# Edge attributes carried through the edge factors' matmul, in a graph block on one core

## The chip, the cores and the metric

One NeuronCore of a Trainium2 chip runs the whole kernel. The metric is the device time in microseconds (us) of one execution, as the median of several. All data are float32 unless a row says otherwise.

## The reference

A graph block of the PaiNN kind, with a residual and a layer norm around it. There are 1250 nodes of 512 numbers (a vector part of 3 x 128, a scalar part of 128) and 40000 edges, sorted by `dst`. `edge_attr` has three numbers for each edge, `edge_weight` is its length r.

```python
x_j = x[src]                                          # a row of 512 for each edge
v_j, s_j = x_j[:, :384].reshape(E, 128, 3), x_j[:, 384:]
s_j = silu(s_j @ W1 + b1) @ W3 + b3                   # 128 -> 384
rbf = sqrt(2 / R) * sin(n * pi * r / R) / r           # n = 1..20
edge_basis = (rbf * cutoff(r)) @ W2 + b2              # 20 -> 384
s1, s2, s3 = split(s_j * edge_basis)
v_msg = v_j * s1[..., None] + s3[..., None] * edge_attr[:, None, :]
x = x + segment_sum(concat([v_msg, s2]), dst)         # first half
x_j = x[src]                                          # second half: a function of
...                                                   # the new x[src] alone, with
x = x + segment_sum(concat([v_2, scal_2]), dst)       # U, V, Wu1, Wu2
return layernorm(x_in + x)
```

## The kernel before

**Preparation.** A node's share of an edge message does not depend on the edge, so the kernel first makes a table in DRAM with one row for each node (`make_rows`, `table_row`; L590 stores it), and a message is the gathered row times the edge's 384 factors. The start also brings indices and weights into the layout that the loop needs. A count of edges that fall out of their windows (L374, cast to an integer at L375, read by the branch at L389) decides between the fast path, `windowed`, and a general one; all here is `windowed`. The attributes are loaded by `load_edges` (L378, issued on the DMA queue of the sync engine, SP; the store's rows name the tile `counts`) and brought to edges-on-partitions by three `turn_attr`: four TensorE transposes each (L284) and a ScalarE copy (L285) into `sh.carried`, which holds four numbers an edge: three attributes and the edge's place in its window of destinations. `sh.attr` is a view of the first three.

**Tiles.** The sorted edges are cut in 79 chunks of 512. Four chunks are a group `g` (20 groups); batch `t` = (group, i) takes the i-th tile of 128 edges of each of the four chunks. There are 80 batches, of which the last two or three are smaller. Each chunk's edges end in a window of 32 destination nodes, so that a sum over edges is a matmul with a one-hot of 128 edges x 32 nodes.

**One batch.**
- GpSimd: `gather(t + 3)`, four indirect DMAs (L743) that bring 4 x 128 table rows into one of five buffers, which the profile names `more` (three of them) and `nodes` (two). The first of the four waits, by a manual dependency, until TensorE has made the factors of batch t + 1.
- TensorE: `edge_factors(t + 1)` (L893) multiplies the transposed basis (`basis_t`, 21 rows: 20 radial functions and a one for the bias) by `w2_sb`, into four PSUM banks `eb`. There is one set of these banks.
- VectorE: `messages(t)`: L903 multiplies the scalar and s3 parts of the gathered rows by the factors in place, L905 the vector part, and with L905 the factors have been read for the last time. Then come the tasks listed under `amid` (among them `make_basis`, L801, `low_counts`, L1017, and one part of `make_turns`, L766); `make_pair` (L926: a one-hot of numbers); and for the batch ahead `make_hot(t + 1)` (L834: the window's one-hot) and `make_spread(t + 1)` (L846: one-hot times the three attributes of `sh.attr`, 3 x 32 columns a tile).
- TensorE: `add_messages(t - 1)` sums with `hot` (L942) and `spread` (L948) into the bank `agg`; `count_links` (L971) multiplies ScalarE's one-hots of the source (L858, L868) by `pair` into the bank `adj`, a count of links between nodes which the second half uses in place of a gather. Spare columns of `adj` hold constants that L766 and L801 read.

Between these, every eighth batch starts the node-wise second half for 128 nodes (products with U, V, Wu1, Wu2), and every fourth closes a group.

**Order.** Each engine runs its instructions in the order of the program. The loop over `t` calls `messages(t)`, the lists `first`, then `add_messages`, `count_links`, `early`, `edge_factors(t + 1)`, `gather(t + 3)`, `mid`, `late`, `dve`. A task is put in a list with a batch and a rank by `at(list, batch, rank, task)`. `count_links` stands ahead of the next `edge_factors` on TensorE, or, in batches with an `amid` task that do not follow a group's last batch (`behind`), after them. A batch after a group's last one, with a `make_basis` among its `amid` tasks too, comes at every eighth: batches 4, 12, 20 and so on.

```python
for t in range(...):
    messages(t)                  # L903, L905, amid, L926, L834, L846
    run(first, t)
    add_messages(t - 1)
    if t not in behind: count_links(t - 1)
    run(early, t)
    made = edge_factors(t + 1)
    gather(t + 3, made)
    if t in behind: count_links(t - 1)
    run(mid, t); run(late, t); run(dve, t)
```

`make_basis` makes the basis of one group ahead (L801), `turn_basis` transposes it (L810) and copies it out of PSUM on ScalarE (L815).

## Time and profile before

| what | value |
| --- | --- |
| median of 3 runs | 491.45 us (491.45, 495.45, 490.73) |
| profiled execution, its own time | 487.85 us |
| its span in the trace | 486.0 us |
| busy: TensorE, VectorE, ScalarE, GpSimd | 402.4, 429.6, 374.4, 344.1 us |
| moved by DMA | 123.29 MB, mean 254 GB/s |
| granted TensorE clock, mean | 0.954 of full speed |

The span is the time from the first to the last record of the profiled execution; its own time is 1.85 us longer. In the rows of the profile `L846 DVE ... x81 | 44.1, 546 | 2.7` is a line of the program, its engine (PE is TensorE, DVE VectorE, ACT ScalarE, POOL GpSimd, SP the sync engine), the number of instructions, their busy time in us, the mean of one in ns, and the idle time in front of them. A row that starts with two numbers is one instruction: its start in us from the start of the span, and its duration in us; what stands in brackets is how long its engine idled ahead of it, and what ended that.

### The profile page before, as it was taken

The page shows a single profiled execution, that of the slowest core. Times are in us where ns is not written, and L with a number is a line of the kernel's source. Part 1 is how long each engine was busy: PE and PEld are TensorE (multiplying, and loading weights), DVE is VectorE, ACT ScalarE, POOL GpSimd, SP SyncE. Part 2 cuts the span into 40 slices and gives each one's busy share as a digit, 9 for nine tenths or more (in the row PEclk, how much of TensorE's full clock was granted, in tenths as well). Part 3 has the DMA queues.
Part 4 walks back from the last instruction along what each step waited for, and adds up shares of the span by engine and source line. Part 5 has one row for each costly group of instructions (what it writes and reads, how often), then busy time and mean ns, then how long its engine had stood idle before and what let it go on. Part 6 is the DMA issues. An engine that isn't in the chain of part 4 may idle for free.

```text
span 486.0 us, 11224 instructions
## 1 busy us (share of the span) xinstructions
PE 402.4 (83%) x4257; PEld 231.4 (48%) x4257; DVE 429.6 (88%) x670; ACT 374.4 (77%) x955; POOL 344.1 (71%) x368
## 2 busy tenths in 40 slices
PE   8537766878869787787888889899899899999992
PEld 6323333444435345444534544554465555555781
DVE  5679799969998998998999899899989989988594
ACT  4486486669859977977986897899789789967672
POOL 9467677777777777777777777777777777781530
PEclk9956798989999999999998999999999999999996
DMA  8988788888888888888888888888888888889023
GB/s 245 325 227 254 228 245 251 252 265 257 276 265 279 276 265 269 269 271 261 269 271 254 290 263 279 264 286 272 282 260 274 270 276 284 264 268 317 6 91 129
DMA packets 37842, 123.29 MB, mean 254 GB/s; under 512 B 7196, under 2 KB 9774, under 8 KB 37778
## 3 DMA queue, kind: packets, MB, share of 16 engines
q0 software_dynamic: 25728, 104.47, 68.9%
q1 hardware_dynamic: 10850, 17.35, 10.7%
q8 instruction: 35, 0.57, 0.5%
q10 hardware_dynamic: 1200, 0.66, 0.5%
q14 instruction: 29, 0.24, 0.2%
HBM read 112.94 MB, written 9.51 MB: 252 GB/s over the span
## 4 chain that ended last, share of the span: by engine, by line
PE 31%; DVE 31%; DMA 13%; POOL 9%; issue 8%; ACT 6%; DVEq 1%; POOLq 0%; SPq 0%
DMA more<-table,src_i 8%; DVE more L905 7%; POOL more L743 6%; PE eb L893 6%; DVE nodes L905 5%; DVE more L903 4%; PE agg L942 4%; DVE nodes L903 4%; PE begun L1346 3%; POOL nodes L743 3%; PE agg L948 3%; PE adj L971 3%; DMA nodes<-in_x_dram 2%; DMA nodes<-table,src_i 2%; ACT one L868 2%
## 5 line engine op out<-in xcount | busy, mean ns | idle before, releaser
L743 POOL DMA_INDIRECT more<-table,src_i x189 | 187.7, 993 | 65.2 <-issue 48.3
L743 POOL DMA_INDIRECT nodes<-table,src_i x124 | 122.9, 991 | 37.8 <-issue 33.5
L868 ACT ACTIVATE one<-one,weight,src_f 128x128 f16<-128x128 f16 x313 | 128.5, 482 | 0.2
L893 PE MATMUL eb<-w_sb,basis_t 21*128 21x384 f32 x614 | 74.1, 551 | 41.7 <-DVE more L905 30.1
L858 ACT ACTIVATE one<-number,low 128x128 f16<-128x128 f16 x313 | 99.8, 392 | 6.9 <-PE adj L971 6.9
L905 DVE TENSOR_TENSOR more<-more,eb 128x1536 f32<-128x1536 f32 (+2 forms) x48 | 81.8, 1705 | 0.0
L903 DVE TENSOR_TENSOR more<-more,eb 128x1024 f32<-128x1024 f32 (+2 forms) x48 | 57.0, 1189 | 15.7 <-PE eb L893 7.3
L893 PEld LDWEIGHTS eb<-w_sb,basis_t 21*128 21x128 f32 x614 | 24.7, 188 | 62.8 <-DVE more L905 39.6
L942 PE MATMUL agg<-more,hot 128*32 128x512 f32 x378 | 54.6, 643 | 0.0
L905 DVE TENSOR_TENSOR nodes<-nodes,eb 128x1536 f32<-128x1536 f32 x30 | 52.5, 1749 | 0.0
L971 PE MATMUL adj<-pair,one 128*128 128x160 f16 x313 | 36.1, 238 | 19.0 <-DVE basis L801 19.0
L948 PEld LDWEIGHTS agg<-more,spread 128*32 128x32 f32 x1134 | 35.3, 116 | 31.9 <-issue 31.0
L903 DVE TENSOR_TENSOR nodes<-nodes,eb 128x1024 f32<-128x1024 f32 x30 | 36.5, 1218 | 11.9 <-PE eb L893 10.0
L846 DVE TENSOR_TENSOR spread<-hot,carried 128x384 f32<-128x384 f32 (+1 forms) x81 | 44.1, 546 | 2.7
L948 PE MATMUL agg<-more,spread 128*32 128x128 f32 x1134 | 42.6, 284 | 0.0
L971 PEld LDWEIGHTS <-one 128*128 128x128 f16 x313 | 22.6, 101 | 35.0 <-issue 33.0
L926 DVE TENSOR_TENSOR pair<-number,column 128x640 f16<-128x640 f16 (+1 forms) x81 | 39.1, 484 | 0.0
L942 PE MATMUL agg<-nodes,hot 128*32 128x512 f32 x248 | 34.1, 605 | 0.0
L948 PEld LDWEIGHTS agg<-nodes,spread 128*32 128x32 f32 x744 | 22.2, 110 | 19.2 <-issue 19.2
L1346 PE MATMUL begun<-upper,cast 128*128 128x512 f32 x57 | 27.8, 487 | 0.4 <-ACT cast L1337 0.4
L815 ACT COPY basis_t<-work 128x512 f32<-128x512 f32 x20 | 11.7, 583 | 20.4 <-PE work L810 20.3
L948 PE MATMUL agg<-nodes,spread 128*32 128x128 f32 x744 | 26.8, 273 | 0.0
(289 smaller groups left out, 687.0 us busy)
## 6 DMA issues: line engine op xcount, KB each, us to landing
table<-more SPq DMA_DIRECT2D x10, 320.0 KB
more<-table,src_i POOLq DMA_INDIRECT x189
spilled<-begun SPq DMA_DIRECT2D x10, 256.0 KB
more<-spilled SPq DMA_DIRECT2D x2, 1280.0 KB
node_x<-in_x_dram SPq DMA_DIRECT2D x35, 64.0 KB
nodes<-table,src_i POOLq DMA_INDIRECT x124
out_dram<-more SPq DMA_DIRECT2D x7, 256.0 KB
nodes<-in_x_dram POOLq DMA_DIRECT2D x2, 768.0 KB
```

The source lines that it names most:

```text
L743: got = nc.gpsimd.indirect_dma_start(out=rows_t[:n, j, :], out_offset=None, in_=sh.table1, in_offset=bass.IndirectOffsetOnAxis(ap=sh.src_i ...
L846: nc.vector.tensor_mul(spread[t][:m, js], hots[t][:m, js, None, :].to_broadcast(shape), sh.attr[:m, g, e : e + n, :, None].to_broadcast(sh ...
L858: nc.scalar.activation(onehots[t][:, j, :], number[:, :P], AF.Abs, bias=low[:, e : e + 1])
L868: nc.scalar.activation(one, one, AF.Relu, scale=less[:, e : e + 1], bias=worth[:, e : e + 1])
L893: made = nc.tensor.matmul(made_in[t][:, j, :V], turned[g][rows, i, :], sh.w2_sb[rows, :], start=True, stop=True,)
L903: nc.vector.tensor_mul(msg[:m, js, V:], msg[:m, js, V:], factors_of(t, js)[:m, :, C:V])
L905: nc.vector.tensor_mul(msg[:m, js, :V].rearrange("p t (k c) -> p t k c", k=3), msg[:m, js, :V].rearrange("p t (k c) -> p t k c", k=3), fac ...
L926: nc.vector.tensor_tensor(pair[:m, js, :].rearrange("p t (l h) -> p t l h", h=2), number[:m, : PARTS * WIN].rearrange("p (l h) -> p l h", ...
L942: nc.tensor.matmul(agg[j * WIN : (j + 1) * WIN, :], hots[t][:, j, :], msg[:, j, :width], start=(i == 0), stop=False, skip_group_check=True,)
L948: nc.tensor.matmul(agg[j * WIN : (j + 1) * WIN, c * C : (c + 1) * C], spread[t][:, j, c, :], msg[:, j, width:], start=False, stop=(i == la ...
L971: nc.tensor.matmul(to[:, :, at : at + WIN], one[:m, j, :], pair[:m, j, :].rearrange("e (p n) -> e p n", n=WIN), start=(i == 0 and j == js[ ...
L1346: nc.tensor.matmul(acc, casts[a, b], rows[:, a, :], start=(start and a == first and k == 0), stop=(stop and a == end - 1 and k == 1),)
```

## The change

- `w2_sb` gets four more columns, `V` to `V + 3`. The rows of features 21 to 24 of each tile hold a one there on the diagonal (`own`), zeros elsewhere.
- `carry(g)` copies the group's `sh.carried` into columns 21 to 24 of the basis, on ScalarE. With that, `edge_factors` has 25 rows in place of 21, 388 columns in place of 384, and the attributes come out behind the factors, in the same PSUM banks.
- `make_spread(t)` reads them there. It stands right behind L905 of its own batch, ahead of `amid`, and no longer a batch ahead; two buffers in place of three. `make_hot` stays a batch ahead.
- At the start the load of the attributes waits until the misses have been counted, and `turn_attr`, with the first `carry`, comes ahead of the first `turn_basis` and of most of the second pass of `floors` (`by_half`).

```diff
-    w2_sb = const.tile([P, V], F32)
+    w2_sb = const.tile([P, V + CARRY], F32)
...
+    nc.vector.scalar_tensor_tensor(
+        own, part, float(-N_RBF - 1), place[:, 2:3], op0=ALU.add, op1=ALU.subtract
+    )
...
-    nc.vector.tensor_copy(missed_i, missed)
+    counted = nc.vector.tensor_copy(missed_i, missed)
     nc.vector.tensor_copy(sh.src_i, sh.src_f)
+    nc.vector.tensor_scalar(w2_sb[:, V:], lane[:, :CARRY], own, None, op0=ALU.is_equal)
     by_tile(ps_front, local_r, 0, 1, sh.local, 1)
-    load_edges(sh.att_r, edge_attr, 3)
+    whole = nc.sync.dma_start(sh.att_r[:full, :], ...)
+    tc.add_manual_dep(
+        whole.ins, counted.ins.name, ...,
+        reason="so that the last rows land first",
+    )
...
+        def carry(g):
+            nc.scalar.copy(basis[:, :, N_RBF + 1 : N_RBF + 1 + CARRY], sh.carried[:, g])
...
         def make_spread(t):
             g, i = batches[t]
+            spread[t] = pool.tile([P, CPG, 3, WIN], F32, name="spread", bufs=2)
+            clear_rest(t, spread[t])
...
                     hots[t][:m, js, None, :].to_broadcast(shape),
-                    sh.attr[:m, g, e : e + n, :, None].to_broadcast(shape),
+                    factors_of(t, js)[:m, :, V : V + 3, None].to_broadcast(shape),
...
-                rows = slice(j * FEAT, j * FEAT + N_RBF + 1)
+                rows = slice(j * FEAT, j * FEAT + N_RBF + 1 + CARRY)
                 made = nc.tensor.matmul(
-                    made_in[t][:, j, :V], turned[g][rows, i, :], sh.w2_sb[rows, :],
+                    made_in[t][:, j, : V + CARRY], turned[g][rows, i, :], sh.w2_sb[rows, :],
...
+            make_spread(t)
             run(amid, t)
             make_pair(t)
-            if t == 0:
-                make_spread(0)
             if t + 1 < NT:
                 make_hot(t + 1)
-                make_spread(t + 1)
...
             at(amid, base + 2, 5, make_basis, g)
+            at(early, base + 2, 7, carry, g)
...
                 at(amid, base + 4, 4, make_basis, g + 1)
+                at(early, base + 4, 7, carry, g + 1)
...
+        next(by_half)
...
+        for k in range(3):
...
+            turn_attr(k, to.rearrange("p (i e) -> p i e", i=TPC))
+        carry(0)
         turn_basis(0)
         for _ in by_half:
             pass
...
-        for k in range(3):
...
-            turn_attr(k, to.rearrange("p (i e) -> p i e", i=TPC))
```

What the orders show. First VectorE, in a batch that makes a basis (batch 12, the first two rows its products; the last row is the next batch's first product). Before:

```order
L903 TENSOR_TENSOR more<-more,eb_384 128x4x256
L905 TENSOR_TENSOR more<-more,eb_384 128x4x384
L801 TENSOR_TENSOR basis<-turn,adj 128x16x20
L926 TENSOR_TENSOR pair<-number,column 128x640
L834 TENSOR_TENSOR hot<-lane,carried 128x128
L846 TENSOR_TENSOR spread<-hot,carried 128x384
L903 TENSOR_TENSOR nodes<-nodes,eb_384 128x4x256
```

The same place with the change, where the lines have the numbers of the changed program (L928 and L930 are the two products, L871 the spread, L826 the basis, L949 the pair, L857 the one-hot):

```order
L928 TENSOR_TENSOR more<-more,eb_388 128x4x256
L930 TENSOR_TENSOR more<-more,eb_388 128x4x384
L871 TENSOR_TENSOR spread<-hot,eb_388 128x384
L826 TENSOR_TENSOR basis<-turn,adj 128x16x20
L949 TENSOR_TENSOR pair<-number,column 128x640
L857 TENSOR_TENSOR hot<-lane,carried 128x128
L928 TENSOR_TENSOR nodes<-nodes,eb_388 128x4x256
```

The spread has moved from behind the one-hot of the next batch to behind the products of its own, ahead of the basis, and it reads `eb`, the factor banks, instead of `carried`.

Second TensorE, from the branch on the misses to the first factors. Before:

```order
L389 TENSOR_LOAD missed_i
L390 COMPARE_AND_BRANCH
L810 MATMUL work<-ident,basis 128x128 x4
L284 MATMUL agg<-ident,counts 128x80 x4
L284 MATMUL begun<-ident,counts 128x80 x4
L284 MATMUL work<-ident,counts 128x80 x4
L893 MATMUL eb_384<-w_sb,basis_t 128x384 x8
```

With the change (L288 are the attributes' transposes, L835 the basis', L918 the factors):

```order
L411 TENSOR_LOAD missed_i
L412 COMPARE_AND_BRANCH
L288 MATMUL agg<-ident,counts 128x80 x4
L288 MATMUL begun<-ident,counts 128x80 x4
L288 MATMUL work<-ident,counts 128x80 x4
L835 MATMUL work<-ident,basis 128x128 x4
L918 MATMUL eb_388<-w_sb,basis_t 128x388 x8
```

The attributes' transposes now stand ahead of the basis' transposes, and through these ahead of the first factors, which follow `basis_t`.

Third ScalarE at the same place, from the last square of the second `floors` on. Before:

```order
L703 ACTIVATE square<-square,shifts 128x320 x2
L815 COPY basis_t<-work 128x512
L703 ACTIVATE low<-src_f,shifts 128x320
L703 ACTIVATE low<-low,shifts 128x320 x2
L712 ACTIVATE src_f<-weight 128x320
L715 ACTIVATE weight<-weight 128x320
L789 COPY adj<-half_n 128x20
L285 COPY carried<-agg 128x4x20x4
L285 COPY carried<-begun 128x4x20x4
L285 COPY carried<-work 128x4x20x4
L796 COPY adj<-fade 128x64
```

With the change (L725 the floors, L289 the attributes' copies, L823 the carry, L840 the basis' copy):

```order
L725 ACTIVATE square<-square,shifts 128x320 x2
L725 ACTIVATE low<-src_f,shifts 128x320
L289 COPY carried<-agg 128x4x20x4
L289 COPY carried<-begun 128x4x20x4
L289 COPY carried<-work 128x4x20x4
L823 COPY basis<-carried 128x16x4
L840 COPY basis_t<-work 128x512
L725 ACTIVATE low<-low,shifts 128x320 x2
L734 ACTIVATE src_f<-weight 128x320
L737 ACTIVATE weight<-weight 128x320
L811 COPY adj<-half_n 128x20
```

The three copies of the attributes and a carry now come ahead of the basis' copy, and one of the floors' steps with them; the other floors and the split of the sources come behind it.

## The prediction

> **What bounds the kernel now.** I read the page's head and groups first, then the waits, then a stretch of the timeline.

> ```profile
> span 486.0 us, 11224 instructions
> ...
> L743 POOL DMA_INDIRECT more<-table,src_i x189 | 187.7, 993 | 65.2 <-issue 48.3
> L743 POOL DMA_INDIRECT nodes<-table,src_i x124 | 122.9, 991 | 37.8 <-issue 33.5
> ```

> ```profile
> 26.28 1.07 POOL L743 DMA_INDIRECT more<-table,src_i  x1 [5.76 <-DMA wu_sb<-in_L_gnn_Wu_dram]
> ...
> 433.87 0.94 POOL L743 DMA_INDIRECT nodes<-table,src_i  x1 [0.30 <-issue]
> ```

> The 313 gathers (189 + 124) fill GpSimd from 26.3 to 434.8 us, 408.5 us of the span. They are busy for 187.7 + 122.9 = 310.6 us; with 0.30 us of issue between two of them that makes 405, so the queue hardly ever stood for another engine. That alone looks like the bound. It is not the only one: the engines that consume the rows are as tight. Line L903, the first product of a batch on VectorE, shows what each of the 78 full batches waited for (total us, times):

> ```profile
>   PE eb L893: 17.3, 13
>   DMA more<-table,src_i: 6.5, 9
>   DMA nodes<-table,src_i: 1.3, 3
> ```

> Thirteen batches started when TensorE's edge factors (`eb`) came, twelve when rows landed, and the other 53 when VectorE itself came free. So three chains take turns: GpSimd's pace, VectorE's own work, and the loop VectorE - TensorE - VectorE through the one set of factor banks. The timeline of batch 36 and the end of batch 35 shows all that the change touches:

> ```profile
> 222.37 0.56 DVE L846 TENSOR_TENSOR spread<-hot,carried 128x384 f32<-128x384 f32 x1
> 222.59 1.15 POOL L743 DMA_INDIRECT more<-table,src_i  x1 [0.30 <-issue]
> ...
> 224.58 1.75 DVE L905 TENSOR_TENSOR more<-more,eb 128x1536 f32<-128x1536 f32 x1
> 225.30 0.95 POOL L743 DMA_INDIRECT nodes<-table,src_i  x1 [0.30 <-issue]
> 226.24 0.48 DVE L801 TENSOR_TENSOR basis<-turn,adj 128x320 f32<-128x320 f32 x1
> 226.64 0.49 DVE L926 TENSOR_TENSOR pair<-number,column 128x640 f16<-128x640 f16 x1
> 226.78 0.44 PE L971 MATMUL adj<-pair,one 128*128 128x160 f16 x4 [2.41 <-DVE basis L801]
> 227.04 0.29 DVE L834 TENSOR_TENSOR hot<-lane,carried 128x128 f32<-128x128 f32 x1
> 227.36 0.56 DVE L846 TENSOR_TENSOR spread<-hot,carried 128x384 f32<-128x384 f32 x1
> ...
> 228.32 0.93 PE L893 MATMUL eb<-w_sb,basis_t 21*128 21x384 f32 x8
> 229.32 1.22 DVE L903 TENSOR_TENSOR more<-more,eb 128x1024 f32<-128x1024 f32 x1 [1.40 <-PE eb L893]
> 230.30 0.95 POOL L743 DMA_INDIRECT nodes<-table,src_i  x1 [0.30 <-PE work L1117]
> ```

> Three things stand in it. A gather that starts while the spread (L846, both inputs in SBUF) is running takes 1.15 us; one that starts inside a product with a PSUM input (L905) takes 0.95. The spread starts 0.03 us after the one-hot (L834) that it reads has ended, where the one-hot started 0.09 us before the end of the pair (L926). And TensorE's link products (L971) wait for L801, which reads the same PSUM bank, with the next factors queued behind them: I call that place **the gate**.

> **The change, part by part.** *Stalls of the gathers.* Taking 0.945 as a free gather, the 313 are 310.6 - 295.8 = 14.8 us too long. I laid every long gather beside the VectorE instruction in whose run it started: 28 of them, from the first to the last below, end with a spread (excess 6.0 us together), 23 with a pair (4.6), 8 with L778 (2.3).

> ```profile
> 37.80 1.09 POOL L743 DMA_INDIRECT more<-table,src_i  x1 [0.30 <-ACT one L858]
> ...
> 431.34 0.97 POOL L743 DMA_INDIRECT nodes<-table,src_i  x1 [0.30 <-issue]
> ```

> With its attributes in PSUM the spread has the operands of L905, which stalls none. Bounds: 0 to -6.0 us on GpSimd; I take -6.0 there, since the operands decide in every pair of rows.

> *Duration of the spread.* Not shown with PSUM; the nearest rows:

> ```profile
> L846 DVE TENSOR_TENSOR spread<-hot,carried 128x384 f32<-128x384 f32 (+1 forms) x81 | 44.1, 546 | 2.7
> L834 DVE TENSOR_TENSOR hot<-lane,carried 128x128 f32<-128x128 f32 (+1 forms) x81 | 22.9, 284 | 0.0
> L1079 DVE TENSOR_TENSOR x<-node_x,work 128x128 f32<-128x128 f32 x9 | 2.5, 279 | 0.0
> ```

> At 128 columns an instruction with one PSUM input (279 ns) takes as long as one without (284). I take no change; bounds -0.02 to +0.03 us apiece, -1.6 to +2.4 us over 81. [...]

> *The gap between one-hot and spread.* The one-hot now comes a batch ahead, so the spread no longer follows what it reads: 0.03 + 0.08 = 0.116 us less VectorE work in each batch. In a batch that VectorE itself bounds, that is time. Of the 73 batches behind the first five, 11 waited for rows and 11 for factors, which leaves 51: 51 x 0.116 = -5.9 us. Bounds 0 (if the wait for the earlier one-hot drains the engine all the same) to -5.9.

> *Later release of the factors.* The spread stands ahead of the release: L905's end is no longer enough, the factors start 0.56 - 0.08 = 0.48 us later. In an ordinary batch this is covered. There they start 0.06 us behind L905 and take 0.93, so they would be ready 1.5 us behind it, while pair, one-hot and spread alone end 1.2 us behind it and most batches carry 0.5 us or more of other VectorE work. At the gate there is no cover: L801 moves behind the spread, L971 with it, and the factors, L903 and the manual wait of the gathers follow, 0.47 us each time:

> ```profile
> PE adj L971 <- DVE basis L801: 19.0, 9, 3.3
> ```

> Nine times 0.47 = +4.2 us. Queued behind L971 on TensorE are the block's U product, two output products and the factors; VectorE waits for these 1.40 us already. Bounds 0 (if rows land last there anyway) to +4.2.

> *What GpSimd's gain is worth.* Only where rows decide: 11 of 73 batches, 11/73 x -6.0 = -0.9 us. It is more if VectorE's chain falls behind no further, up to the whole 6.0.

> *Carries.* Twenty small copies on ScalarE, priced by the row of the same 64 columns, 0.30 us:

> ```profile
> 33.53 0.30 ACT L796 COPY adj<-fade 128x64 f32<-128x64 f32 x1
> ACT basis_t L815 <- PE work L810: 20.3, 14, 3.0
> ```

> Six us in all. Behind each stands the transposed basis' copy, ahead of which ScalarE idles 20.3 us in 14 waits; that hides them. Without that cover they would cost at most 6. Four more columns on 384 add 1% to 0.93 us, nothing that shows; two spread buffers suffice, as TensorE uses the spread of two batches ago ahead of the factors it needs.

> *The start.* Here the attributes join the path.

> ```profile
> 20.54 0.44 SPq L137 DMA_DIRECT2D counts<-in_edge_attr_dram  x1
> 21.94 0.15 DVE L375 CAST missed_i<-missed 1x1 int32<-1x1 f32 x1 [0.28 <-PE missed L374]
> 26.53 1.08 PE L810 MATMUL work<-ident,basis 128*128 128x128 f32 x4 [4.20 <-DVE basis L801]
> 27.63 0.81 PE L284 MATMUL agg<-ident,counts 80*128 80x80 f32 x4
> 27.65 0.58 ACT L815 COPY basis_t<-work 128x512 f32<-128x512 f32 x1 [0.97 <-PE work L810]
> 28.73 1.16 ACT L703 ACTIVATE low<-low,shifts 128x320 f32<-128x320 f32 x2
> 29.91 0.49 DVE L708 SCALAR_TENSOR_TENSOR weight<-square,low 128x320 f32<-128x320 f32 x1 [0.48 <-ACT low L703]
> 31.94 0.70 ACT L285 COPY carried<-agg 128x320 f32<-128x320 f32 x1
> 32.99 0.73 ACT L285 COPY carried<-work 128x320 f32<-128x320 f32 x1
> 34.31 1.22 DVE L903 TENSOR_TENSOR more<-more,eb 128x1024 f32<-128x1024 f32 x1 [2.44 <-DMA more<-table,src_i]
> ```

> The load now goes out behind L375, at 22.15 instead of 20.54, and has the queues more to itself, since the table's last rows are ahead of it. It landed at 27.6; I take 27.8, bounds 26.8 to 29.2 (the same 7.1 us after issue). From there: first transposes 0.9, three copies 1.8, a carry 0.3, the basis transposes 1.1 and their copy 0.6 with small hand-overs make 4.8; then the source floors on ScalarE, which now stand behind that copy, 1.1; then L708 to the first one-hot on VectorE, 2.0. L903 of batch 0 comes 7.9 us after the landing, at 35.7, 1.4 later than 34.31, though rows may land 1 us earlier. Batch 0 then does one spread instead of two (-0.6), batch 1 saves its gap (-0.1), and the factors of batch 3, on whose chain TensorE then runs, start 0.47 later: **+1.2 us**, bounds 0 to +2.6. The other loads queued behind the held one on SyncE are first read 20 us later.

> *Sum.* -5.9 + 4.2 - 0.9 + 1.2 = -1.4 us. The profiled execution took 487.85 us (span 486.0 and 1.85 around it), so 486.45; it lies 3.6 under the median shown, 491.45, which gives 490.05, rounded **490.0**.

> **The rivals.** *GpSimd's pace decides* (faster): gathers wait for nothing but issue in nearly all rows, so the 6.0 us may come through whole if the gate is covered. For it, the small sum of other waits; against it, the gather at 230.30 starts only 1.05 us behind the factors it is tied to, 0.75 over its issue, and the factors move 0.47. Result -6.0 + 1.2 = -4.8: 486.65.

> *Nothing is relieved, the gate stays* (slower): TensorE's L971 waits for L801, now behind the spread, nine times 0.47, and the spread keeps its gap because it still waits on VectorE's own count, and the stalls merely move to pairs. It decides once a batch's spare time ahead of L903 is under 0.47, as at 229.32, where it is negative. +4.2 + 1.2 = +5.4: 496.85. Against it: the one-hot it waits for has ended 3 us before.

> *The spread is not what stalls the gathers* (so the change does not do what it is made of): then GpSimd gains nothing and -5.9 + 4.2 + 1.2 = -0.5: 490.95. For it only that long gathers also end with pairs; against it the rows at 222.59 and 225.30. [...]

> **How the numbers follow.** Forecast 0.55, GpSimd's pace 0.20, nothing relieved 0.10, spread not the cause 0.12, else 0.03. The forecast's own bounds are its start (0 to 2.6) and the spread's length (-1.6 to 2.4), about 487.2 to 493.8. The range reaches down past the faster rival, to 485.0, and up to 495.0, short of the slower one. About 1% (4.9 us) is what a measurement of this kernel can tell from no change: faster than 486.5 half of the second case and a little of the first, 0.19; slower than 496.4 most of the third, 0.08; within, 0.73.

> **What would show it.** Right: no gather ends with a spread, and their mean falls from 0.99 to about 0.97; L926 starts before the spread's end; the waits of L971 for L801 grow by 0.47 apiece; the first L903 stands near 35.7. Wrong: gathers at 0.99 as before; spreads at 0.60 or more; waits of L903 for the factors grown in ordinary batches too (17.3 us to over 30); a first L903 beyond 37; many gathers waiting for the factors instead of issue.

## The result, and the profile after

The changed kernel takes 493.9 us (median of 22 runs, 489.5 to 498.95), the one before 490.93 (22 runs beside them): 1.0061 times as long, 95% interval 1.004 to 1.0083, so **3.0 us slower**. The forecast was 1.4 us faster. Three of the seven groups of experiments were measured at times when every kernel, the one before included, took 563 to 592 us; they are read against their own kernel before and decide nothing here. It does not belong to certain chips: the one numbered 15 gave 565 us for the kernel before in one group and 490 us in another. What the other groups show is that the new place of the spread, ahead of the basis in nine batches, costs more than the rest of the change saves.

The page's head and groups of the changed kernel (line, engine, operation, count | busy us, mean ns | idle before):

```profile
span 493.4 us, 11248 instructions
...
L765 POOL DMA_INDIRECT more<-table,src_i x189 | 188.2, 996 | 71.9 <-issue 48.1
L765 POOL DMA_INDIRECT nodes<-table,src_i x124 | 121.1, 976 | 39.2 <-issue 32.3
...
L871 DVE TENSOR_TENSOR spread<-hot,eb 128x384 f32<-128x384 f32 (+1 forms) x78 | 42.3, 543 | 0.0
```

The spread reads PSUM at the price it had with SBUF (543 ns, 546 before). The gathers have hardly gained: 188.2 + 121.1 = 309.3 us busy, 310.6 before. Laid beside VectorE's instructions as in the prediction, no long gather starts in the run of a spread now (28 did before; the 31 that still start there take at most 0.949 us). But the excess over 0.945 us each is 13.5 us, 14.8 before: 9 long gathers now start in a one-hot (L857; 2.8 us, before 5 with 0.4 us), 13 in a pair (3.8 us), 6 in the node-wise addition L1107 (2.0 us).

The waits (us, times, longest) show where the time went:

```profile
PE adj L994 <- DVE basis L826: 18.4, 9, 2.3
DVE nodes L928 <- PE eb L918: 17.0, 9, 3.5
DVE more L928 <- PE eb L918: 16.0, 15, 3.1
POOL more L765 <- PE eb L918: 12.6, 9, 2.9
```

The first product of a batch waits for its factors 33.0 us in 24 batches, 17.3 us in 13 before, and the gathers, which waited for factors 3.5 us in 4 waits before, now do so for 12.6 us in 9. From the first gather to the last the changed kernel takes 416.3 us, 7.8 more than before: stalls 1.3 less, waits of the queue 9.1 more (2.9 of them up to 62 us).

Its gates, in the timeline. The first is batch 28, the second batch 36; the last rows of each piece are the next batch's first product:

```profile
185.60 1.22 DVE L928 TENSOR_TENSOR nodes<-nodes,eb 128x1024 f32<-128x1024 f32 x1
186.73 1.75 DVE L930 TENSOR_TENSOR nodes<-nodes,eb 128x1536 f32<-128x1536 f32 x1
...
188.39 0.56 DVE L871 TENSOR_TENSOR spread<-hot,eb 128x384 f32<-128x384 f32 x1
188.85 0.49 DVE L826 TENSOR_TENSOR basis<-turn,adj 128x320 f32<-128x320 f32 x1
...
189.40 0.44 PE L994 MATMUL adj<-pair,one 128*128 128x160 f16 x4 [2.28 <-DVE basis L826]
...
191.60 1.68 PE L918 MATMUL eb<-w_sb,basis_t 25*128 25x388 f32 x8
...
193.34 1.22 DVE L928 TENSOR_TENSOR nodes<-nodes,eb 128x1024 f32<-128x1024 f32 x1 [3.39 <-PE eb L918]
193.58 0.94 POOL L765 DMA_INDIRECT more<-table,src_i  x1 [1.56 <-PE eb L918]
```

```profile
228.46 1.22 DVE L928 TENSOR_TENSOR more<-more,eb 128x1024 f32<-128x1024 f32 x1
...
234.80 1.22 DVE L928 TENSOR_TENSOR more<-more,eb 128x1024 f32<-128x1024 f32 x1 [1.99 <-PE eb L918]
```

The same starts in the kernel before:

```profile
182.67 1.22 DVE L903 TENSOR_TENSOR nodes<-nodes,eb 128x1024 f32<-128x1024 f32 x1
...
188.54 1.22 DVE L903 TENSOR_TENSOR nodes<-nodes,eb 128x1024 f32<-128x1024 f32 x1 [1.39 <-PE eb L893]
```

```profile
223.45 1.21 DVE L903 TENSOR_TENSOR more<-more,eb 128x1024 f32<-128x1024 f32 x1
```

From batch 36 to 37 the changed kernel falls back by (234.80 - 228.46) - (229.32 - 223.45) = 0.47 us, as worked out ahead; so it does at batches 52, 60 and 68. From batch 28 to 29 it loses 7.74 - 5.87 = 1.87: there the factors alone took 1.68 us instead of 0.93. The stretches of 3.41 us around it (us, busy of each engine with counts, granted clock in the third column from the end) say why:

```profile
core 0: us, PE busy (x) PEld busy (x) DVE busy (x) ACT busy (x) POOL busy (x), PEclk, DMA share, GB/s
183.30:186.71 3.41, 2.99 (x41) 1.60 (x44) 3.41 (x6) 3.41 (x11) 2.59 (x3) 1.00 0.88 264
186.71:190.13 3.42, 1.14 (x24) 0.97 (x17) 3.24 (x6) 1.29 (x5) 2.71 (x3) 1.00 0.86 272
190.13:193.54 3.41, 3.41 (x15) 1.67 (x14) 0.20 (x1) 3.02 (x8) 1.58 (x2) 0.50 0.72 217
193.54:196.96 3.42, 3.42 (x26) 1.85 (x29) 3.42 (x4) 2.03 (x6) 2.77 (x3) 0.50 0.65 194
196.96:200.37 3.41, 3.41 (x43) 2.49 (x36) 2.77 (x6) 2.18 (x6) 1.95 (x3) 1.00 0.84 253
```

TensorE worked 1.14 us of the second stretch, a third of it, as it waited for L826; in the next two it was granted half its clock. In this trace three gates went so. The kernel before has the same idle at its gates, but in its profiled execution the stretches fell otherwise: its mean clock of 0.954 is above that of all 71 runs of it beside the experiments (0.915 to 0.952, mean 0.937; the changed kernel's mean is 0.938). So the two profiles differ by 7.3 us, the medians by 3.0.

### The profile page after: what moved, and what is told of

The parts are those of the page before. It is cut to its first block, busy times and chain, and to the rows that moved or that the text cites. A ratio compares the mean times of both kernels' runs of the same rounds, so it can differ in the third digit from the quotient of the medians.

```text
span 493.4 us, 11248 instructions
## 1 busy us (share of the span) xinstructions
PE 412.2 (84%) x4257; PEld 236.3 (48%) x4257; DVE 421.2 (85%) x672; ACT 377.6 (77%) x975; POOL 342.0 (69%) x368
## 3 DMA queue, kind: packets, MB, share of 16 engines
q1 hardware_dynamic: 10850, 17.35, 10.6%
## 4 chain that ended last, share of the span: by engine, by line
PE 32%; DVE 26%; DMA 9%; POOL 7%; issue 7%; ACT 5%; DVEq 0%; POOLq 0%
DVE more L930 6%; PE eb L918 6%; PE agg L965 5%; DMA nodes<-table,src_i 5%; DMA more<-table,src_i 4%; DVE nodes L930 4%; DVE more L928 4%; POOL nodes L765 4%; POOL more L765 4%; PE agg L971 3%; DVE spread L871 3%; PE begun L1369 3%; DVE nodes L928 2%; PE adj L994 2%; ACT one L893 2%
## 5 line engine op out<-in xcount | busy, mean ns | idle before, releaser
L765 POOL DMA_INDIRECT more<-table,src_i x189 | 188.2, 996 | 71.9 <-issue 48.1
L765 POOL DMA_INDIRECT nodes<-table,src_i x124 | 121.1, 976 | 39.2 <-issue 32.3
L893 ACT ACTIVATE one<-one,weight,src_f 128x128 f16<-128x128 f16 x313 | 128.5, 482 | 0.2
L918 PE MATMUL eb<-w_sb,basis_t 25*128 25x388 f32 x614 | 77.6, 575 | 38.6 <-DVE spread L871 37.8
L930 DVE TENSOR_TENSOR more<-more,eb 128x1536 f32<-128x1536 f32 (+2 forms) x48 | 81.8, 1707 | 0.0
L928 DVE TENSOR_TENSOR more<-more,eb 128x1024 f32<-128x1024 f32 (+2 forms) x48 | 57.1, 1191 | 20.1 <-PE eb L918 16.0
L928 DVE TENSOR_TENSOR nodes<-nodes,eb 128x1024 f32<-128x1024 f32 x30 | 36.6, 1219 | 22.1 <-PE eb L918 17.0
L918 PEld LDWEIGHTS eb<-w_sb,basis_t 25*128 25x128 f32 x614 | 25.6, 195 | 60.4 <-DVE spread L871 52.5
L930 DVE TENSOR_TENSOR nodes<-nodes,eb 128x1536 f32<-128x1536 f32 x30 | 52.5, 1749 | 0.0
L994 PE MATMUL adj<-pair,one 128*128 128x160 f16 x313 | 36.1, 238 | 18.4 <-DVE basis L826 18.4
L971 PEld LDWEIGHTS agg<-more,spread 128*32 128x32 f32 x1134 | 35.2, 115 | 31.4 <-issue 31.2
L971 PE MATMUL agg<-more,spread 128*32 128x128 f32 x1134 | 42.5, 283 | 0.0
L871 DVE TENSOR_TENSOR spread<-hot,eb 128x384 f32<-128x384 f32 (+1 forms) x78 | 42.3, 543 | 0.0
L949 DVE TENSOR_TENSOR pair<-number,column 128x640 f16<-128x640 f16 (+1 forms) x81 | 38.6, 477 | 0.0
L965 PE MATMUL agg<-nodes,hot 128*32 128x512 f32 x248 | 35.8, 634 | 0.0
L971 PEld LDWEIGHTS agg<-nodes,spread 128*32 128x32 f32 x744 | 23.0, 113 | 20.7 <-issue 20.3
L840 ACT COPY basis_t<-work 128x512 f32<-128x512 f32 x20 | 11.7, 585 | 20.8 <-PE work L835 20.8
L971 PE MATMUL agg<-nodes,spread 128*32 128x128 f32 x744 | 27.5, 278 | 0.0
```

Source lines behind the costliest of these rows:

```text
L765: got = nc.gpsimd.indirect_dma_start(out=rows_t[:n, j, :], out_offset=None, in_=sh.table1, in_offset=bass.IndirectOffsetOnAxis(ap=sh.src_i ...
L871: nc.vector.tensor_mul(spread[t][:m, js], hots[t][:m, js, None, :].to_broadcast(shape), factors_of(t, js)[:m, :, V : V + 3, None].to_broad ...
L893: nc.scalar.activation(one, one, AF.Relu, scale=less[:, e : e + 1], bias=worth[:, e : e + 1])
L918: made = nc.tensor.matmul(made_in[t][:, j, : V + CARRY], turned[g][rows, i, :], sh.w2_sb[rows, :], start=True, stop=True,)
L928: nc.vector.tensor_mul(msg[:m, js, V:], msg[:m, js, V:], factors_of(t, js)[:m, :, C:V])
L930: nc.vector.tensor_mul(msg[:m, js, :V].rearrange("p t (k c) -> p t k c", k=3), msg[:m, js, :V].rearrange("p t (k c) -> p t k c", k=3), fac ...
```

## The experiments

All ratios are to the kernel before, run beside each; intervals are 95%.

**The basis first at the gates.**

```diff
-            make_spread(t)
+            if t % 8 != 4:
+                make_spread(t)
             run(amid, t)
+            if t % 8 == 4:
+                make_spread(t)
```

> The changed kernel, but at the nine gates (every eighth batch, from batch 4) the basis L826 stands ahead of the spread again. Gate theory (the spread ahead of the basis holds TensorE's link products, and with them the next factors, 0.47 us nine times): about 4 us come back, ratio to the kernel before 0.997 to 0.999, and the first product's waits for factors fall from 33 us to some 28. Release theory (factors released 0.47 us later cost time in ordinary batches too): 1 us or less comes back, ratio 1.004 to 1.006, waits stay at 30 or more. Clock theory (the time went to stretches in which TensorE is granted half its clock, after it idled): the gate's idle of 2.25 us gets shorter by 0.47, so fewer low stretches; the ratio follows the granted clock, about 2.5 us for each 0.01 of the mean.

> The changed kernel, with the basis L826 ahead of the spread again at the nine gates. It ran once while rows landed some 3 us later than usual in every kernel (565 us for the kernel before); here it is to run beside rows that land as in the profile. Gate theory: about 4 us come back, ratio 0.997 to 0.999. Release theory (ordinary batches pay for the later release): 1 us or less comes back, 1.004 to 1.006.

Measured: 1.0009 (0.9963 to 1.0055) in a group at 565 us; 488.13 us, **0.9933 (0.99 to 0.9966)** in one at 491. Against the changed kernel that is 1.28% or 6.3 us; the two intervals put together leave some 4.3 to 8.2. The release theory falls; the gate theory holds, with its 4 us if anything too small. The clock has a part in it: its mean over the runs rose from 0.938 to 0.945, which by the slope of the last section (2.3 us for each 0.01) is 1.6 us, an estimate; with the 4.2 us that makes 5.8. So ordered, the kernel is 3.3 us (1.7 to 4.9) faster than the one before: all else in the change does save time, though less than the 5.6 us forecast for it (5.9 + 0.9 - 1.2). Waits for factors fell to 26.3 us:

```profile
DVE more L928 <- PE eb L918: 14.9, 11, 3.1
DVE nodes L928 <- PE eb L918: 11.4, 8, 3.5
```

**The spread from SBUF, in its new place.**

```diff
-                    factors_of(t, js)[:m, :, V : V + 3, None].to_broadcast(shape),
+                    sh.attr[:m, g, e : e + n, :, None].to_broadcast(shape),
```

> The changed kernel, but the spread, in its new place, reads the attributes from SBUF; the factors are released by L930 again, the attributes are still carried in PSUM and not read. Gate theory: L826 still stands behind the spread, so the 4 us stay, and the gathers' stalls by the spread (6 us of GpSimd) come back: ratio 1.006 to 1.012. Release theory: ordinary batches recover, ratio 1.000 to 1.003, waits for factors back to 20 us or less. If neither the release nor the stalls matter, 1.006 as before.

> The changed kernel, with the spread in its new place and its attributes from SBUF, so that L930 releases the factors again and the spread may stall gathers again. Release theory: first products wait for factors 20 us or less, ratio 1.000 to 1.003. Gate theory: L826 is still behind the spread, 1.006, and up to 6 us of stalls come back on GpSimd: 1.006 to 1.012.

Measured: 1.0127 (1.0076 to 1.0179) in a group at 565 us; 496.9 us, **1.0118 (1.0089 to 1.0146)**, slower than with PSUM although the factors are released earlier. The page's rows:

```profile
L765 POOL DMA_INDIRECT more<-table,src_i x189 | 189.7, 1003 | 70.3 <-issue 48.1
L765 POOL DMA_INDIRECT nodes<-table,src_i x124 | 125.7, 1014 | 39.7 <-issue 32.9
...
L871 DVE TENSOR_TENSOR spread<-hot,carried 128x384 f32<-128x384 f32 (+1 forms) x81 | 43.6, 540 | 0.0
```

The gathers are busy for 315.4 us, 6.1 more than with PSUM; 23 long ones start in a spread's run again (4.4 us of excess), and those in a pair have 7.9 us, 3.8 with PSUM. So in these two kernels, which differ in the one operand, the operands do stall them; by what way, no run here shows. And the waits for factors stayed, 32.3 us in 21 batches, though they are released earlier: they do not come from the release. A small gain by the earlier release, hidden under the stalls, is not excluded. The spread's own duration does not tell the two apart: 543 ns with PSUM, 540 with SBUF.

**Filling the gates.** Six products that nothing reads, while TensorE waits for the basis; in the changed kernel, then in the one before:

```diff
                 add_messages(t - 1)
+                if t % 8 == 4 and t < 72:
+                    filled = work()
+                    for _ in range(6):
+                        nc.tensor.matmul(filled[:, :P], ident, ident, start=True, stop=True)
```

> The changed kernel with six products of the identity (128 x 128, never read) on TensorE at each of the nine gates, between the sums of the batch before and the link products, where TensorE idles 2.25 us. Clock theory (windows of 3.41 us in which TensorE works under about half of the time are followed by half its clock; three of the gates were in the profile, 6.8 us each at half the clock, 2.5 us lost each): the gates no longer lower the clock, granted mean up from 0.931 to 0.95 or more, and 4 to 7 us come back: ratio 0.992 to 0.998. Gate and release theory: nothing comes back, 1.006, or a little more if the products end behind L826.

> The kernel before with the same six unread products on TensorE at each of the nine gates. The fill was worth 1.3% to the changed kernel (1.0061 to 0.9931). If half-clock stretches cost all kernels alike: about as much here, ratio 0.987 to 0.990. If they cost only where the factors have lost their slack by their later release (an execution's time falls by 2.3 us for each 0.01 of granted clock in the changed kernel, by 0.6 us in the one before): the clock rises by some 0.02 here too, but the time falls by 1 to 2 us, ratio 0.996 to 0.998.

> The kernel before with six unread products on TensorE at each of the nine gates, on a chip where rows land as in the profile, if it is one. If half-clock stretches cost all kernels alike: ratio 0.987 to 0.990, as much as in the changed kernel. If they cost only where the later release has taken the factors' slack: the granted clock rises by some 0.02, the time falls by 1 to 2 us, 0.996 to 0.998.

Measured: the changed kernel 487.81 us, **0.9931 (0.9897 to 0.9965)**, mean clock 0.962; the kernel before **0.9884 (0.982 to 0.9948)**, mean clock 0.955, a ratio from four runs only (1.0348, 1.0299 to 1.0398, in a group at 565 us). The timeline of the changed kernel at the gate of batch 28:

```profile
182.99 1.22 DVE L928 TENSOR_TENSOR nodes<-nodes,eb 128x1024 f32<-128x1024 f32 x1 [0.77 <-PE eb L918]
...
184.50 1.60 PE L1744 MATMUL work<-ident 128*128 128x128 f32 x12
...
186.25 0.48 DVE L826 TENSOR_TENSOR basis<-turn,adj 128x320 f32<-128x320 f32 x1
...
186.79 0.44 PE L994 MATMUL adj<-pair,one 128*128 128x160 f16 x4 [0.68 <-DVE basis L826]
...
188.33 0.93 PE L918 MATMUL eb<-w_sb,basis_t 25*128 25x388 f32 x8
...
189.33 1.22 DVE L928 TENSOR_TENSOR nodes<-nodes,eb 128x1024 f32<-128x1024 f32 x1 [1.99 <-PE eb L918]
```

The fill ends ahead of the basis and delays nothing; the factors take 0.93 us at full clock, and L928 comes 2.99 us behind the spread's end (186.34) instead of 4.39. So the half-clock stretches at the gates cost about 1% of either kernel (1.0061 to 0.9931, and 1 to 0.9884). That also says that they are no difference between the two: my theory that only the changed kernel pays for them, because the later release took its slack, falls. The same batch of the kernel before, filled:

```profile
182.29 1.21 DVE L903 TENSOR_TENSOR nodes<-nodes,eb 128x1024 f32<-128x1024 f32 x1
...
188.16 1.22 DVE L903 TENSOR_TENSOR nodes<-nodes,eb 128x1024 f32<-128x1024 f32 x1 [1.40 <-PE eb L893]
```

In these two traces no gate falls into a half-clock stretch, so the gate's own price can be read: batch 28 takes 189.33 - 182.99 = 6.34 us in the changed kernel and 188.16 - 182.29 = 5.87 in the one before. Over the nine gate batches it is 55.0 us against 50.75, or 4.25 more, as forecast.

**Order and fill together** (both edits in the changed kernel).

> The changed kernel with the basis ahead of the spread at the gates and the nine gates filled. Each alone gave 0.993. If the basis' earlier place helped mostly through the clock (a shorter idle), the two do not add: 0.991 to 0.994. If the basis is worth its 0.47 us nine times whatever the clock, and the fill the clock: they add, 0.982 to 0.986.

> The changed kernel with the basis ahead of the spread at the gates and the gates filled, where rows land as in the profile, if the chip does so. Each alone gave 0.993. Same cause (both shorten the idle that halves the clock): 0.991 to 0.994. Two causes: 0.982 to 0.986. Where rows land late the fill costs 2 us a gate (1.0336).

Measured: 486.11 us, **0.9885 (0.9848 to 0.9922)** (1.0336 in a group at 565 us). Beside the fill the basis' order is worth 0.46%, 2.3 us, with an interval of some 2.5 on both sides; without it, 6.3. Whether the fill takes part of the order's gain is not settled; 4.2 us lies within reach of both. The two fastest kernels cannot be told apart: filled, the kernel before stands at 0.9884. With gates filled and the basis first, the rest of the change moves 0.0 us, with some 3.6 on both sides, where 5.6 us of saving were forecast. The first products wait for factors no longer than in the kernel before with its gates filled: 17.2 us in 14 batches against 17.7 in 15.

**No wait at the gates**: the basis reads its cut-off factors from SBUF.

```diff
-                fading.pop(g)[:, :, None].to_broadcast([P, EPG, N_RBF]),
+                fade[:, g * EPG : (g + 1) * EPG, None].to_broadcast([P, EPG, N_RBF]),
```

> The changed kernel, but the basis L826 reads its cut-off factors from SBUF instead of the spare columns of the link bank, so that TensorE's link products wait for no basis at the nine gates. Gate theory: the wait of 18.4 us is gone, the factors start behind the spread also there, up to 9 x 1.5 = 13 us at most, some of which waits for rows take: ratio 0.980 to 0.995. Release theory: only the gates' own part, 4 us, comes back: 0.997. If gathers stalled by the basis (two SBUF inputs, 18 of them at most 0.4 us each) or late rows eat it: 1.000 to 1.006. Clock theory: the gates' idle is gone, the mean clock is at 0.95 or more.

Measured: 489.03 us, **0.9952 (0.9923 to 0.9981)**. Its waits:

```profile
DVE more L928 <- DMA more<-table,src_i: 9.1, 9, 2.1
DVE nodes L928 <- DMA nodes<-table,src_i: 7.0, 8, 1.6
DVE more L928 <- PE eb L918: 6.6, 7, 2.6
DVE nodes L928 <- PE eb L918: 5.5, 5, 3.5
```

Waits for factors are down from 33.0 to 12.1 us, waits for rows up from 8.8 (5.0 + 3.8) to 16.1, and 7.8 us of waits for other TensorE results are new. Taking the link products' 18.4 us of waiting away bought about 5: behind it stood the gathers and other work of TensorE. The mean clock, expected at 0.95 or more, was 0.943.

**The gap alone**, in the kernel before:

```diff
-            make_pair(t)
             if t == 0:
                 make_spread(0)
             if t + 1 < NT:
                 make_hot(t + 1)
+            make_pair(t)
+            if t + 1 < NT:
                 make_spread(t + 1)
```

> The kernel before, but the pair stands between the one-hot and the spread, so that the spread no longer follows at once the one-hot it reads; nothing else. It measures the gap of 0.116 us alone. If VectorE bounds most batches, as the prediction took it: 51 x 0.116 = 5.9 us less, ratio 0.988. If VectorE's saving is given back in waits for rows or factors: 0.996 to 1.000. At gates the pair that TensorE's link products read comes 0.28 us later, but L801 is waited for longer only if the pair is late: at most 2.5 us more, 1.005.

> The kernel before with the pair between one-hot and spread: the gap of 0.116 us alone. As the prediction took it (51 x 0.116): 0.988. If half of it or more is given back as waits for rows and factors: 0.994 to 0.998. With late rows it was 0.9964 (0.9929 to 0.9999).

> The kernel before with the pair between one-hot and spread, where rows land as in the profile, if the chip does so. The prediction's term, 51 x 0.116 us: 0.988. Half or more of it given back as waits for rows and factors: 0.994 to 0.998. Where rows land late it moved nothing (0.9964 and 1.0016).

Measured: 0.9964 (0.9929 to 0.9999) and 1.0016 (0.9982 to 1.005) in groups at 565 us; 493.92 us, **1.0052 (1.001 to 1.0094)**, where the prediction's term meant 0.988. Page and waits:

```profile
L743 POOL DMA_INDIRECT more<-table,src_i x189 | 190.6, 1009 | 65.9 <-issue 48.8
L743 POOL DMA_INDIRECT nodes<-table,src_i x124 | 122.3, 986 | 37.8 <-issue 35.7
```

```profile
DVE more L903 <- DMA more<-table,src_i: 12.1, 13, 2.0
DVE nodes L903 <- DMA nodes<-table,src_i: 1.7, 4, 0.6
```

Waits for rows rose from 7.8 us to 13.8, waits for factors from 17.3 to 21.6, and the gathers got 2.3 us longer, as those in spreads and pairs, which now follow each other, are stalled more (excess 14.1 us, 10.6 before). From batch 5 to 76 VectorE was busy 6.2 us less and idle 10.2 us more: its saving became waiting. Not all of the +2.6 us need be the new order: the mean clock of these runs was 0.924, that of the runs beside them 0.936, which at 1.2 us for each 0.01 in the kernel before is about 1.4 us, an estimate.

**More work for GpSimd**, in the kernel before: a memset behind each batch's gathers, one column wide, then 192.

```diff
+        idle = pool.tile([P, 192], F32, name="idle", bufs=1)
...
             clear_rest(t, rows_t, nc.gpsimd)
+            nc.gpsimd.memset(idle, 0.0)
```

> The kernel before with one more small instruction on GpSimd behind each batch's four gathers (a memset of one column that nothing reads, 0.10 us by the profile's rows of that size, some 0.1 to 0.2 us with its issue). If GpSimd's pace sets the time, as the sum of gathers, stalls and issue says (waits in it only 0.6 us after the first 62 us): 80 times 0.1 to 0.2 us, ratio 1.016 to 1.033. If GpSimd counts only in the batches that wait for rows, as the prediction took it (11 of 73): 1 to 2 us, 1.002 to 1.004.

> As the run before it, with the memset 192 columns wide. The narrow one (0.117 us) lay inside the 0.30 us that the queue leaves between two gathers anyway: in its trace a gather still starts 0.30 us behind the last. A memset of 192 columns takes about 0.25 us by the profile's row of that size, and with the 0.19 us behind it the space between two batches' gathers grows from 0.30 to 0.44: 78 x 0.13 = 10 us. If GpSimd's pace sets the time: ratio 1.015 to 1.021. If it counts only in the batches that wait for rows (11 of 73): 1.003. In between: the other engines leave that much slack on average.

Measured: narrow 0.9995 (0.9959 to 1.0031), wide 494.67 us, **1.0102 (1.0035 to 1.0169)**. The narrow one took 0.118 us inside the 0.30 us between gathers, and tells nothing. The wide one in the timeline:

```profile
226.23 0.95 POOL L744 DMA_INDIRECT more<-table,src_i  x1 [0.30 <-issue]
227.17 0.28 POOL L758 MEMSET idle<- 128x192 f32 x1
227.61 0.95 POOL L744 DMA_INDIRECT nodes<-table,src_i  x1 [0.16 <-issue]
```

The space grows from 0.30 to 0.44 us, 9.8 us over the kernel, and the time by 5.0 (1.7 to 8.3): about half of GpSimd's time is time of the kernel, by the middle of a wide interval (0.17 to 0.85): not all, and more than 11 in 73 (0.15).

**The start alone**, in the kernel before: the attributes' load held behind `counted`, `turn_attr` and one floors step ahead of `turn_basis(0)`, as in the diff of the change, without the carry.

> The kernel before with the start of the changed one alone: the attributes' load held behind the count of misses, their transposes ahead of the basis' transposes, one floors step ahead. Start theory (the prediction's +1.2 us, bounds 0 to 2.6): ratio 1.0025, first L903 near 35. If the later start also shifts TensorE's work into more half-clock stretches up to 60 us: 2 to 3 us, 1.005. If the first batches make it up: 1.000.

> The kernel before with the changed one's start alone. Prediction's term: +1.2 us, 1.0025. If later factors of the first batches fall into more half-clock stretches: 1.005. If the first batches make it up: 1.000. With late rows it was 1.0014 (0.9981 to 1.0047).

Measured only in groups at 565 us: 1.0014 (0.9981 to 1.0047) and 0.999 (0.9952 to 1.0028). The first product came at 35.09 and 35.18 us, close to what was expected, but no cost shows in the time; where the kernel takes 491 us it stays unmeasured.

**Fills at the start too**: in the changed kernel with order and fill, seven more unread products ahead of the factors of batch 1 and eight ahead of those of batch 3.

> The changed kernel with the basis first at the gates, the nine gates filled, and two more fills at the start: seven unread products behind the first factors, where TensorE idles 4.6 us, and eight ahead of the factors of batch 3, where it idles 4.1 us. In the kernel without these two the clock was half until 44 us and again from 51 to 58 us, and full to 477 us; gathers waited 4.6 us in that stretch. If the idle there is what lowers the clock: full from some 40 us on, 2 to 3 us less, ratio 0.982 to 0.986. If the first batches wait for VectorE's own work: no change, 0.988. Where rows land late, the nine fills alone cost 2 us each (1.034).

Measured only in a group at 571 us: 591.72 us, 1.0345 (1.0309 to 1.0381), as the nine fills alone there. It decides nothing on the start.

For the groups at 565 to 571 us my expectations blamed late rows. The traces do not bear that out: ScalarE, VectorE and GpSimd there are released within some 0.3 us of each other, about 1.5 us behind the last record of the TensorE work that they wait for (in the first run with the basis first they start at 300.33, 300.42 and 300.66 us, that record ends at 299.05), a batch takes 6.1 us instead of 5.1 (medians), and a fill costs 2 us a gate. What is late there was not settled.

## Why the prediction was wrong, step by step

- **The gap: the step that failed.** "In a batch that VectorE itself bounds, that is time", 51 x 0.116 = -5.9 us. VectorE's work per batch did fall as worked out, but the gap alone, undone in the kernel before, gave +2.6 us (0.5 to 4.6), not -5.9. The 53 batches that started when VectorE came free were counted as VectorE's (four of them in fact waited for other TensorE results, 2.1 us). Where VectorE came last, the rows had landed a median of 1.0 us earlier (under 0.5 us in 10 of the 45 batches whose landing can be told). That covers 0.116 us in one batch, but the savings of many batches add up, and the rows come from a queue that hardly stopped (405 of 408.5 us, by the prediction's sum) and did not get faster by them (gathers of 312.9 us in that run, 310.6 before). So, as I read it, what one chain gives up the next takes: waits for rows went from 7.8 to 13.8 us. The changed kernel itself says the same less sharply. Gap, rows and start were to bring -5.9 - 0.9 + 1.2 = -5.6 us; with the gate's order undone they brought -3.3 (-4.9 to -1.7), and between the two filled kernels 0.0 (3.6 on both sides). So a part of the saving may come through there; how much of it is the gap's no run isolates.
- **The gate: right mechanism, upper bound too low.** +4.2 us was forecast. The timeline shows 0.47 a gate where the clock was full, 4.25 us over nine in the filled kernels; undoing the order gave 6.3 (4.3 to 8.2), or 2.3 beside the fill. "Bounds 0 to 4.2" left out that a gate can be followed by a lower clock (0.50 behind that of batch 28, which lost 1.87 us instead of 0.47). Of the 4.4 us by which the forecast missed, 2.1 are this (6.3 in place of 4.2) and 2.3 the savings that fell short (3.3 in place of 5.6).
- **The stalls: right operand, wrong sum.** No long gather starts in a spread, as forecast, and SBUF in the same place costs 6.1 us of gathers. But the queue has hardly a free moment (before, gathers of 310.6 us and 0.30 us of issue between two fill 405 of 408.5 us), and gathers that no longer meet a spread meet other instructions: 9 long ones in a one-hot had 2.8 us of excess, before 5 with 0.4. GpSimd gained 1.3 us, not 6.0.
- **What GpSimd's time is worth.** 11/73 was taken, about half was measured. Half of 1.3 is 0.7 us, the forecast had 0.9: two errors that cancel, by luck.
- **The spread's duration, the carries, ordinary release:** right. 543 ns a spread and 249 ns a carry (forecast 300); in the kernel with the earlier release the factors were waited for no less (32.3 us in 21 batches), and with basis first and gates filled no more than in the kernel before (17.2 and 17.7 us).
- **The start.** The first L928 came at 35.50, forecast 35.7. The two rows of the timeline:

```profile
27.51 0.77 PE L288 MATMUL agg<-ident,counts 80*128 80x80 f32 x4 [5.12 <-DMA counts<-in_edge_attr_dram]
...
35.50 1.22 DVE L928 TENSOR_TENSOR more<-more,eb 128x1024 f32<-128x1024 f32 x1 [0.22 <-DMA more<-table,src_i]
```

  By batch 2 it is 0.59 us behind the kernel before. From there to batch 5 another 1.7 us go, partly in a half-clock stretch (50 to 60 us), so +1.2 is neither shown nor refuted.
- **The rivals.** "GpSimd's pace decides" was nearer in its mechanism than the forecast, and wrong in what it would bring, as the stalls moved. "Nothing is relieved, the gate stays" gave 496.85 with a chance of 0.10; its parts are near what was measured: gate in full, stalls that "merely move to pairs", and a gap without worth in the run that isolates it, though for another reason, as VectorE's work did fall. The measured 3.0 us lies between it and nothing. A sum with gap 0, stalls -0.7, gate +4.2 and start +1.2 gives +4.7, above the 2.0 to 4.1 of the measurement: some saving is missing in it.
- **The signs named.** "Waits of L903 for the factors ... (17.3 us to over 30)" came true, at 33.0, but not from the release in ordinary batches: with the basis first they fell to 26.3, with the fills too to 17.2. "Gathers at 0.99 as before" came true as well (0.988), and so did gathers that wait for factors (12.6 us). One sign of being right failed: the waits of the link products for the basis did not grow, 18.4 us against 19.0.

## What to carry to other kernels

Where several engines are each busy to within a few tenths of a microsecond of a batch, a count of "who came last" does not price a saving: add or take a known time on one engine and see how much of it comes through. Here the gathers' stalls by the spread (6.0 us of excess) went when its operand moved to PSUM, and stalls by other instructions came in their place (13.5 us of excess in all, 14.8 before), on a queue that had hardly a free moment. And when an instruction is put ahead of another, ask who waits for the second one; undoing that order in nine batches of eighty turned 1.0061 into 0.9933.
